# Rows loaded in one burst, x in four buffers, stores on a second queue: the end of a four-layer graph network on one core

## The chip, the cores and the metric

The kernel runs on one NeuronCore of one Trainium2 chip. The metric is the time of one execution on the device, in microseconds (us). Engines are named as the profile names them: PE is the matrix engine, DVE the vector engine, ACT the scalar engine, POOL is GpSimd, and SP is the sync engine, which here only issues transfers (DMAs).

## The reference

Eight graphs' node features `x` (8 batches of 2048 nodes with 64 features) pass through four layers that share one adjacency matrix. Each layer normalises x, applies ReLU, computes something of the graph, and adds it to x. The change lies in the last layer, which is graph attention, and above all in its last step:

```python
h = jnp.maximum(_layernorm(x, axis=-1), 0.0)
# _L3_gnn_ref(h, adj, weight, a, bias):
adj = adj.at[jnp.diag_indices(N)].set(1.0)
h = jnp.einsum('bni,io->bno', x, weight)
e_src = h @ a[:D, 0]
e_dst = h @ a[D:, 0]
e = jax.nn.leaky_relu(e_src[:, :, None] + e_dst[:, None, :], negative_slope=ALPHA)
e = adj[None, :, :] * e
attention = jax.nn.softmax(e, axis=-1)
h_prime = jnp.einsum('bij,bjd->bid', attention, h)
return h_prime + bias
# the last line of the whole network:
x = x + _L3_gnn_ref(...)
```

## The kernel before

**Layout.** x is held transposed: features of two batches on the 128 partitions, nodes along the free axis. So there are four pairs of batches (`NP = 4`), and the 2048 nodes are cut into four chunks (`NC = 4`) of 512 (`CW`), each of four tiles (`TC = 4`) of 128 nodes. One chunk of x is 128 x 4 x 512 floats, 1 MB. Between layers it lies in DRAM, in `xs[3][0..3]` for the last layer.

**The last layer.** For inputs such as these the kernel takes the branch `layer3_near`. In the last step of layer 2 the class `Scores` has already left, for every node, its projected features and two scores per batch in DRAM (`f_rows`, 2112 bytes a node; stored by SP at L1895 and L1896). The nodes are sorted by their number of neighbours, in an order read at the start of the layer (`order`, L1933). The class `Near` then goes over 15 tiles of 128 sorted nodes (`others`): POOL gathers the rows of each node and of its neighbours from `f_rows` into `ring` (L1959), DVE works out weights and multiplies, PE sums in PSUM, DVE divides. A sixteenth tile, that of the nodes with most neighbours, is done densely beside them (`first_tile`): its adjacency rows are gathered (L2060), ACT works out its exponentials, PE sums. What a tile gives is written by POOL to its nodes' places in DRAM, in `att_rows` (`put_back`, L1970).

**The end.** `result` (L2141) brings this back. Once all of `att_rows` is written, it loads 16 tiles of rows (`att(t)`, 128 x 512 floats, 256 KB each, L2150), transposes each by four PE instructions into PSUM (`pt`, two buffers, L2153), and adds it and the bias to x by one DVE instruction (L2155). When a chunk's four tiles are done, four stores of 256 KB take it to the output (L2159). x comes chunk by chunk into two halves of one buffer (L2145, L2146), so chunks 2 and 3 take the places of chunks 0 and 1. All these transfers are issued from SP, one after another.

**Memory.** `slots` hands out named stretches of SBUF, q0 to q5, of 16 KB a partition, that live through the whole kernel and are used again and again under new names: the end's x is in q2, its rows in q0 and q1. `w` is the last layer's own pool (`att`); its tiles lie one after another where layers 0 to 2 had theirs, and `ring` alone takes 76 KB a partition of it.

**Order of the work.** The tile framework sets the order of the instructions on each engine when it builds the program; it need not be that of the source. An engine then runs its own list strictly in order, and an instruction that waits holds up all behind it on that engine, transfers included. Semaphores between engines are placed by the framework from the tiles that instructions read and write.

Of the kernel before, what the change touches and what calls it, by code (L numbers as in the profile page):

```python
# [7 lines left out]
F = mybir.dt.float32  # L8
# [11 lines left out]
P = 128  # L20
# [3 lines left out]
NP = NB // 2  # L24
NT = N // P
R = P // NP
CW = 512
NC = N // CW
# [18 lines left out]
class Slots:  # L47
# [3 lines left out]
    def __init__(self, pool):  # L51
        self.flat = {f"q{i}": pool.tile([P, 2 * N], F, name=f"q{i}") for i in range(6)}
        self.pool = None
# [42 lines left out]
class Kernel:  # L96
# [1421 lines left out]
    def layer3_near(self, slots):  # L1518

        tc = self.tc
        with (
            tc.tile_pool(reuse_waits="tile", name="att", bufs=1) as w,
            tc.tile_pool(reuse_waits="tile", name="att_ps", bufs=1, space=PSUM) as ps,
        ):
            near = Near(self, slots, w, ps)
            first = near.first_tile()  # L1530
            others = near.others()
            next(first)
            next(others)
            for _ in range(12):
                next(first)
            for part in others:
                next(first, None)
            for part in first:
                pass
            near.put_back()  # L1540
            near.result()
# [369 lines left out]
class Near:  # L1911
# [5 lines left out]
    def __init__(self, kern, slots, w, ps):  # L1917
        self.kern, self.nc, self.w, self.ps = kern, kern.nc, w, ps
        nc = self.nc
        *_, self.y, self.total, self.rows = kern.last_slots(slots)  # L1920
        self.turn = 0
        self.x = slots.tile([P, 2, NP, CW], F, name="x_end", tag="q2")
        two = slots.tile([P, 2, N], F, name="first_row", tag="q0")
        self.row, self.whole = two[:, 0], two[:, 1].bitcast(I32)

        self.m = slots.tile([P, 4, NB, P], F, name="m", tag="q0")

        self.att = Halves(slots, "att", ("q0", "q1"), True)
        two = slots.tile([P, 2, N], F, name="first_at", tag="q1")
        self.first_at = two[:, 0].rearrange("p (t n) -> p t n", t=NT)  # L1930
        self.on_all = two[:, 1].rearrange("p (i b n) -> p i b n", i=2, b=NB)
        self.order = w.tile([P, 2, NT], I32, name="order")
        nc.sync.dma_start(self.order, kern.orders[1])  # L1933
        self.near = w.tile([P, FIRST[NT]], I32, name="near")
        nc.vector.tensor_scalar(self.near, kern.near, 1.0, -1.0, op0=OP.max, op1=OP.add)
        self.there = w.tile([P, FIRST[NT]], F, name="there")
        nc.vector.tensor_scalar(self.there, kern.near, 0.0, None, op0=OP.is_gt)
        self.ring = w.tile([P, self.RING, WIDE], F, name="ring")
        self.at, self.unread, self.back = 0, (), []
# [201 lines left out]
    def result(self):  # L2141

        nc, w, kern = self.nc, self.w, self.kern
        for ch in range(NC):
            x = self.x[:, ch % 2]  # L2145
            nc.sync.dma_start(x, kern.xs[3][ch])  # L2146
            for i in range(TC):
                t = ch * TC + i
                r = self.att(t)
                nc.sync.dma_start(r, kern.att_rows[t * P : (t + 1) * P])  # L2150
                pt = self.ps.tile([P, 4, P], F, name="pt", bufs=2)
                for q in range(NP):
                    nc.tensor.transpose(pt[:, q], r[:, q * P : (q + 1) * P], kern.ident)  # L2153
                here = x[:, :, i * P : (i + 1) * P]
                nc.vector.scalar_tensor_tensor(  # L2155
                    here, pt, kern.col("bias3"), here, op0=OP.add, op1=OP.add
                )
            for q in range(NP):
                nc.sync.dma_start(kern.a["out"][q, :, ch * CW : (ch + 1) * CW], x[:, q])  # L2159


def kernel(tc, a):
# [94 lines left out]
```

## Time and profile before

| What | us |
|---|---|
| median of 3 runs | 2223.89 (2223.14 to 2229.41) |
| the profiled execution | 2223.47 |
| its span in the profile | 2221.7 |
| PE busy | 1967.9 (89%) |
| DVE busy | 1115.2 (50%) |
| POOL busy | 727.9 (33%) |
| ACT busy | 708.9 (32%) |
| first gather of the last layer | 1929.7 |
| last write to `att_rows` issued | 2173.8 |
| first row load of `result` issued | 2176.65 |
| last output store issued | 2212.5 |

All times of instructions are counted from the start of the span. The span is what the profiler saw of the one execution; 1.8 us of the execution's own time lie around it. A line L135 in the profile is a helper through which nearly all matrix products go. Lines that begin with a time are the timeline: start, duration, engine, line, operation, and in brackets how long the engine was idle before it and what ended that. SPq is SP's list of transfers; a duration there is that of issuing them, and transfers next to one another are merged into one line with a count. A table by stages gives, for each stretch, every engine's busy time with its number of instructions, the clock that PE was granted, the mean busy share of the 16 DMA engines, and what they moved.

### The profile page before, as it was taken

The page shows a single profiled execution, that of the slowest core. Times are in us where ns is not written, and L with a number is a line of the kernel's source. Part 1 is how long each engine was busy: PE and PEld are TensorE (multiplying, and loading weights), DVE is VectorE, ACT ScalarE, POOL GpSimd, SP SyncE. Part 2 cuts the span into 40 slices and gives each one's busy share as a digit, 9 for nine tenths or more (in the row PEclk, how much of TensorE's full clock was granted, in tenths as well). Part 3 has the DMA queues.
Part 4 walks back from the last instruction along what each step waited for, and adds up shares of the span by engine and source line. Part 5 has one row for each costly group of instructions (what it writes and reads, how often), then busy time and mean ns, then how long its engine had stood idle before and what let it go on. Part 6 is the DMA issues. An engine that isn't in the chain of part 4 may idle for free.

```text
span 2221.7 us, 21410 instructions
## 1 busy us (share of the span) xinstructions
PE 1967.9 (89%) x7530; PEld 1187.1 (53%) x7530; DVE 1115.2 (50%) x1980; ACT 708.9 (32%) x1347; POOL 727.9 (33%) x609
## 2 busy tenths in 40 slices
PE   5877899987879989999999998998999999679873
PEld 1454766652226766353353532876777666345432
DVE  7846767744762032524425244988302222349762
ACT  6401455543444342020110200433434333258300
POOL 0012066755320002726537175011000000277760
PEclk8856899996777989999999998999999999789996
DMA  8231133451122453040130402456333443375655
GB/s 318 71 101 27 52 94 112 126 159 67 38 76 86 131 130 118 0 139 13 54 99 0 114 1 82 149 191 218 103 123 123 144 151 124 131 199 164 180 158 201
DMA packets 107742, 253.76 MB, mean 114 GB/s; under 512 B 19600, under 2 KB 19744, under 8 KB 100320
## 3 DMA queue, kind: packets, MB, share of 16 engines
q1 hardware_dynamic: 90000, 185.22, 26.1%
q0 software_dynamic: 17616, 67.00, 10.1%
q8 instruction: 63, 1.03, 0.2%
q14 instruction: 63, 0.52, 0.1%
HBM read 218.37 MB, written 33.81 MB: 114 GB/s over the span
## 4 chain that ended last, share of the span: by engine, by line
PE 57%; DVE 8%; POOL 7%; DMA 6%; issue 5%; ACT 3%; SPq 1%; POOLq 0%; DVEq 0%; ACTq 0%
PE pp L135 25%; PE pk L135 16%; PE bank L135 4%; POOL ring L1959 3%; PE acc L135 3%; PE pn L135 2%; PE p L135 2%; POOL q L1794 1%; DVE q L1809 1%; DMA q<-in_adj_dram,order 1%; POOL dt L632 1%; DMA adj_t<-in_adjT_dram 1%; PE pd L135 1%; PE po L135 1%; DMA ring<-f_rows,near 1%
## 5 line engine op out<-in xcount | busy, mean ns | idle before, releaser
L294 ACT CAST adj<-adj_t 128x512 fp32r<-128x512 f32 x384 | 236.7, 619 | 718.3 <-PE pp L135 625.2
L1353 POOL TENSOR_TENSOR acc<-acc,y 128x512 f32<-128x512 f32 x224 | 277.4, 1271 | 444.9 <-DVE y L1348 444.9
L135 PE MATMUL pk<-q,w 128*128 128x512 f32 (+1 forms) x1024 | 358.2, 612 | 9.9 <-DVE w L1270 8.9
L135 PEld LDWEIGHTS pk<-q,w 128*128 128x128 f32 (+1 forms) x1024 | 136.6, 188 | 228.0 <-issue 179.1
L135 PE MATMUL acc<-q,ident 128*128 128x512 f32 x416 | 205.1, 620 | 30.0 <-DVE q L2049 19.1
L1348 DVE SCALAR_TENSOR_TENSOR y<-pk,bias,q 128x512 f32<-128x512 f32 x224 | 157.7, 746 | 139.9 <-PE pk L135 130.3
L135 PE MATMUL pp<-adj,u_n_hi 128*128 128x512 f32 x768 | 217.2, 402 | 0.0
L135 PE MATMUL pp<-adj,u_n_lo 128*128 128x512 f32 x768 | 214.2, 398 | 0.0
L135 PEld LDWEIGHTS pp<-adj,u_n_hi 128*128 128x128 f32 x768 | 143.4, 188 | 39.0 <-issue 5.9
L1959 POOL DMA_INDIRECT ring<-f_rows,near x121 | 141.4, 1169 | 69.2 <-issue 57.4
L135 PEld LDWEIGHTS pp<-adj,u_n_lo 128*128 128x128 f32 x768 | 144.6, 188 | 34.5
L135 PEld LDWEIGHTS acc<-q,ident 128*128 128x128 f32 x416 | 77.1, 196 | 106.3 <-issue 48.8
L2063 POOL IOTA q<- 128x2048 int32 x1 | 1.8, 1835 | 355.3 <-PE p L135 355.3
L1794 POOL TENSOR_TENSOR q<-q,beta 128x512 f32<-128x512 f32 x57 | 67.6, 1188 | 104.8 <-DVE beta L1770 81.6
L135 PE MATMUL pp<-adj,x_ind_hi 128*128 128x512 f32 x256 | 95.5, 489 | 2.1 <-DVE q L700 1.9
L1348 DVE SCALAR_TENSOR_TENSOR acc<-pk,bias,q 128x512 f32<-128x512 f32 x32 | 22.6, 746 | 143.6 <-PE pk L135 143.6
L135 PE MATMUL bank<-std,from_rows 32*128 32x512 f32 x128 | 47.7, 938 | 41.8 <-DVE std L242 33.8
L135 PE MATMUL pp<-adj,h_n_hi 128*128 128x512 f32 x256 | 77.7, 416 | 0.0
L135 PE MATMUL pp<-adj,h_n_lo 128*128 128x512 f32 x256 | 75.3, 407 | 0.0
L2030 DVE TENSOR_TENSOR q<-ring,e 128x1024 f32<-128x1024 f32 x58 | 69.9, 1217 | 9.9 <-PE acc L135 9.7
L135 PE MATMUL pp<-adj,ah_n_hi 128*128 128x512 f32 x256 | 73.1, 405 | 0.0
L1416 DVE TENSOR_TENSOR q<-pn,later 128x512 f32<-128x512 f32 x32 | 21.5, 687 | 101.6 <-PE pn L135 101.4
(382 smaller groups left out, 3216.7 us busy)
## 6 DMA issues: line engine op xcount, KB each, us to landing
adj_t<-in_adjT_dram SPq DMA_DIRECT2D x160, 512.0 KB, 3.8
rows<-in_adj_dram SPq DMA_DIRECT2D x16, 1024.0 KB, 5.6
adj_t<-in_adjT_dram SPq DMA_DIRECT2D x64, 256.0 KB, 3.0
q<-x SPq DMA_DIRECT2D x12, 1024.0 KB, 5.0
q<-in_embT_dram SPq DMA_DIRECT2D x8, 1024.0 KB, 12.2
x<-q SPq DMA_DIRECT2D x8, 1024.0 KB, 3.9
x_ch<-in_xT_dram SPq DMA_DIRECT2D x4, 1024.0 KB, 6.2
h_rows<-q SPq DMA_DIRECT2D x16, 256.0 KB, 2.9
```

The costliest lines, as they stand in the source:

```text
L135: self.nc.tensor.matmul(out, lhsT, rhs, start=start, stop=stop)
L294: nc.scalar.copy(moving, at[:, i])
L632: nc.gpsimd.tensor_sub(dt, th[0], th[1])
L1348: nc.vector.scalar_tensor_tensor(y, pks[b, half], bias[:, b : b + 1], emb[:, b], op0=OP.add, op1=OP.mult,)
L1353: nc.gpsimd.tensor_add(acc, acc, y)
L1416: nc.vector.tensor_add(to, pn, later[:, 2].unsqueeze(1).to_broadcast(full))
L1794: self.nc.gpsimd.tensor_tensor(x, x, by.unsqueeze(2).to_broadcast([P, NB, D]), op=OP.mult)
L1809: nc.vector.tensor_add(d, d, self.pas.pop(i - 1))
L1959: self.nc.gpsimd.indirect_dma_start(to, None, self.kern.f_rows[:], bass.IndirectOffsetOnAxis(ap=index, axis=0))
L2030: nc.vector.tensor_tensor(y.rearrange("n i (b f) -> n i b f", b=NB), block[:, i : i + 2, : NB * D].rearrange("n i (b f) -> n i b f", b=NB) ...
L2063: nc.gpsimd.iota(whole, pattern=[[1, N]], base=0, channel_multiplier=0)
```

## The change

Four edits are made, all in the last layer. First, `result` issues the loads of all 16 tiles of rows ahead of its loop over chunks, not one by one inside. Second, x gets four buffers: the two halves in q2 as before, and a second tile of the same size, `x_more`, 16 KB a partition, which is allocated from `w` ahead of that pool's other tiles. Third, the four loads of x move from `result` to `layer3_near`, behind the first steps of the dense tile. They remain on SP. Fourth, the output is stored from ACT's queue and no longer from SP's.

```diff
@@ layer3_near
             next(others)
             for _ in range(12):
                 next(first)
+            for ch in range(NC):
+                tc.nc.sync.dma_start(near.x[ch], self.xs[3][ch])
             for part in others:
                 next(first, None)
             for part in first:
@@ Near.__init__
         *_, self.y, self.total, self.rows = kern.last_slots(slots)
         self.turn = 0
-        self.x = slots.tile([P, 2, NP, CW], F, name="x_end", tag="q2")
+        x = slots.tile([P, 2, NP, CW], F, name="x_end", tag="q2")
+        more = w.tile([P, 2, NP, CW], F, name="x_more")
+        self.x = [x[:, 0], x[:, 1], more[:, 0], more[:, 1]]
         two = slots.tile([P, 2, N], F, name="first_row", tag="q0")
@@ Near.result
         nc, w, kern = self.nc, self.w, self.kern
+        for t in range(NT):
+            nc.sync.dma_start(self.att(t), kern.att_rows[t * P : (t + 1) * P])
         for ch in range(NC):
-            x = self.x[:, ch % 2]
-            nc.sync.dma_start(x, kern.xs[3][ch])
+            x = self.x[ch]
             for i in range(TC):
                 t = ch * TC + i
                 r = self.att(t)
-                nc.sync.dma_start(r, kern.att_rows[t * P : (t + 1) * P])
                 pt = self.ps.tile([P, 4, P], F, name="pt", bufs=2)
@@
             for q in range(NP):
-                nc.sync.dma_start(kern.a["out"][q, :, ch * CW : (ch + 1) * CW], x[:, q])
+                nc.scalar.dma_start(kern.a["out"][q, :, ch * CW : (ch + 1) * CW], x[:, q])
```

## The prediction

> **What bounds the kernel now.** I read the page first, for the span and the chain of work that ended last.
>
> ```profile
> span 2221.7 us, 21410 instructions
> ...
> PE 57%; DVE 8%; POOL 7%; DMA 6%; issue 5%; ACT 3%; SPq 1%; POOLq 0%; DVEq 0%; ACTq 0%
> ```
>
> PE carries 57% of the chain, in layers 0 to 2, which the change does not touch. It can act at two places: at the end, where `result` runs, and at the start of the last layer, where the loads of x are to go. For the end I took SP's timeline from 2176 us on, then the table by stages.
>
> ```profile
> 2176.65 4.90 SPq L2150 DMA_DIRECT2D q<-att_rows  x9
> 2184.97 5.44 SPq L2159 DMA_DIRECT2D out_dram<-q  x8
> 2190.58 0.45 SPq L2146 DMA_DIRECT2D q<-x  x1
> 2191.07 1.92 SPq L2150 DMA_DIRECT2D q<-att_rows  x3
> 2193.83 0.32 SPq L2146 DMA_DIRECT2D q<-x  x1
> 2194.19 1.47 SPq L2150 DMA_DIRECT2D q<-att_rows  x2
> 2202.51 1.80 SPq L2159 DMA_DIRECT2D out_dram<-q  x4
> 2204.36 1.25 SPq L2150 DMA_DIRECT2D q<-att_rows  x2
> 2210.97 2.01 SPq L2159 DMA_DIRECT2D out_dram<-q  x4
> ```
>
> SP's list is strictly in order, and here it makes the steps of the end. The last scatter into `att_rows` lands at 2176.5 and row loads begin at once, nine of them. Then SP stands at the stores of chunk 0 until DVE has made them (2184.97), and goes on to the stores of chunk 1. Only behind these do x's chunk 2 (2190.58), three rows, chunk 3 (2193.83), two rows; the last two rows wait behind chunk 2's stores until 2204.36.
>
> ```profile
> 2180.00:2185.00 5.00, 4.32 (x18) 3.01 (x17) 3.00 (x4) 0.00 (x0) 0.00 (x0) 0.50 0.98 349
> 2185.00:2190.00 5.00, 3.38 (x17) 2.38 (x16) 2.91 (x4) 0.00 (x0) 0.00 (x0) 0.78 0.76 284
> 2190.00:2195.00 5.00, 0.00 (x0) 0.00 (x0) 0.00 (x0) 0.00 (x0) 0.00 (x0) 0.56 1.05 309
> 2195.00:2200.00 5.00, 1.35 (x7) 1.38 (x8) 0.97 (x2) 0.00 (x0) 0.00 (x0) 0.50 0.99 377
> 2200.00:2205.00 5.00, 3.58 (x15) 2.48 (x13) 2.78 (x4) 0.00 (x0) 0.00 (x0) 0.50 0.75 289
> 2205.00:2210.00 5.00, 1.84 (x9) 1.57 (x8) 1.41 (x2) 0.00 (x0) 0.00 (x0) 0.50 0.60 193
> 2210.00:2215.00 5.00, 0.16 (x1) 0.00 (x0) 0.84 (x2) 0.00 (x0) 0.00 (x0) 0.50 0.61 210
> ```
>
> PE and DVE do nothing from 2190 to 2195: rows are queued behind stores. The DMA engines are not idle then (share 1.05): they load the two chunks of x. Their share falls to 0.6 after 2205. The DMA view from 2176 to 2216 gives the rate:
>
> ```profile
> q1 hardware_dynamic: 4873, 10.45, 75.1%
> ```
>
> 10.45 MB in 75.1% of 40 us, so 30.0 us of all engines: **348 GB/s while busy**. In one-us slices the last busy one ends near 2215.2, where the last store lands. The remaining 6.5 us to 2221.7 are the program's end.
>
> For the other place, SP's timeline around 1906 and the one of all engines from 1925:
>
> ```profile
> 1906.10 12.35 SPq L2146 DMA_DIRECT2D q<-x  x2
> ...
> 1925.45 0.38 SPq L1896 DMA_DIRECT2D f_rows<-scores  x1
> 1925.89 0.93 SPq L1933 DMA_DIRECT2D order<-order  x1
> ```
>
> ```profile
> 1929.69 0.95 POOL L1959 DMA_INDIRECT ring<-f_rows,near  x1 [28.42 <-issue]
> ...
> 1937.03 2.35 DVE L2067 SCALAR_TENSOR_TENSOR q<-q,own 128x2048 f32<-128x2048 int32 x1 [8.35 <-DMA q<-in_adj_dram,order]
> 1937.21 2.99 POOL L1959 DMA_INDIRECT ring<-f_rows,near  x1 [0.30 <-issue]
> ```
>
> The two loads at 1906.10 (L2146; the second from 1918.0) are x's chunks 0 and 1. So these are early already; only chunks 2 and 3 can be gained by "early". SP waits there 11.6 us for DVE to finish with q2's second half, ahead of the last stores into `f_rows`. Tiles of `w` come later: `order` is the first of SP's, after the last `f_rows` store, and DVE's first work in `w` follows its last of layer 2 (1924.97 after 1924.90). POOL's first gather follows at 1929.69.
>
> **What the Trainium skill says.** (1) "DMA: Bandwidth & Descriptors", section "Issuing engines are not separate DMA queues": transfers from SP, ACT and POOL run on the same 16 engines, so another queue saves the sequencer's issue time only. Before has no transfer on ACT, so the sharing is unseen; SP's issue time is 446 ns at the median for a store and 464 for a row. What ACT's queue can also save here is the waiting ahead of the rows. (2) The same page, "Specifications", has about 358 GB/s as a core's share of memory bandwidth; the 348 above agree, so I take the end as bounded by bytes. (3) Its "Queues, rings and completion order": an engine takes turns between queues, packet by packet. So stores on ACT's queue slow the rows still loading on SP's, and loads of x on SP's slow POOL's gathers. No trace of before shows two such queues full together. (4) "SBUF — State Buffer", "SBUF: two separate sides": DVE and GpSimd share a port pair as a lock. The trace agrees: the gather at 1937.21 takes 2.99 us for a usual 0.95 while DVE's L2067 (2.35 us) runs. It is not a sign of full DMA queues, and moves with L2067.
>
> **The end, part by part.** Bytes left after 2176.5: rows 16 x 262,144 = 4.19 MB and stores as much, 8.39 MB. The two chunks of x, 2.10 MB, are gone from here. Four pace-setters:
> - DMA: 8.39 MB / 348 GB/s = 24.1 us. The first row reaches PE at 2179.3, and its own 0.75 us at that rate put the start of the flow near 2178. Without a break the last byte lands at 2202.1.
> - PE and DVE: the first eight rows start on DVE from 2180.44 to 2187.9, 1.07 us apart (PE at half clock 1.0, DVE 0.75 beside it). Sixteen: 2180.44 + 15 x 1.07 + 0.75 = 2197.2.
> - SP: 16 x 0.464 = 7.4 us, to 2184.1, ahead of the need.
> - ACT: idle at the end (0.00 in every stage); four stores behind the last DVE work, 4 x 0.446 = 1.8 us, and 2.7 us to land: 2201.7.
>
> Do the rows come in time under sharing? Until 2184.5 they have the engines alone: 2.26 MB, nearly nine rows. Then chunk 0's stores take half and a row lands every 1.5 us: row 15 near 2195, when PE wants it at 2195.3. No wait of size. DMA then sets the end with 2202.1; I add 1 us for gaps, as nothing starts a store before its DVE work. With 6.5 us behind it, 2209.6 in place of 2221.7: **12.1 us saved**. Half of it is x's 2.10 MB (6.0 us), the rest idle DMA time.
>
> The row loads wait for the last scatter as before, so "together" gains nothing at 2176.65. In the program as built, SP's transfers use eight completion semaphores in turn, and each waits for the one eight earlier. With stores from ACT in the same turn, a late row may wait for a store: from 0 to some 3 us more; I take 0, since PE and DVE pace those rows anyway.
>
> **The start of the last layer.** Chunks 0 and 1 keep their place, since q2's halves come free as before. `x_more` lies in `w`, so I expect its two loads on SP right behind `order`, at about 1926.9: 2 x 0.32 us of issue, with nothing queued behind them on SP until the rows at 2176. Their 2.10 MB run 6.0 us, until about 1934.5, beside POOL's first gathers. POOL issues one each 1.26 us and doesn't wait for landings of 3.9 us. Who waits is DVE: L2067 starts at 1937.03 when the dense tile's adjacency rows (1 MB, issued 1930.95) land. Of the 6.0 us, some 3.6 are over when these begin to flow; the rest shares by halves: about 2.4 us late. DVE is idle in 8.8 us of the 10 from 1970 to 1980, waiting for gathers, and the chain runs through POOL's issues there; that cover takes it up. Bounds: 0 and 6.0 us (all of it exposed); I take 0.6. `ring` and the rest of `w` move up by 16 KB; as they wait for the end of layer 2 already, I cost this at 0, between minus and plus 1.
>
> Sum: 12.1 - 0.6 = 11.5 us. From the profiled execution's 2223.47 that gives 2212.0; the median of the runs is 0.42 above it, so **2212.4 us**.
>
> **Rivals.**
> - *The early loads are exposed.* Should they stand ahead of `order` or of the last `f_rows` stores in SP's list, POOL's start is late by their 6.0 us and nothing takes that up: 2218.4. For it: SP already puts x ahead of `f_rows`. Against: `w` opened late in before.
> - *The end has holes.* Stores cut the rows to half their rate for longer and semaphores hold late rows; PE waits, and the last stores slip by 5 us: about 2217.4. For it: the rate under two queues is unseen.
> - *Slower: the last layer is laid out otherwise.* The interleaving of the dense tile with the 15 others is fixed at build, and new transfers and another memory layout may shift it. The stage lasts 247 us and holds single waits of 12.1 us (DVE's L2004, ending 1985.8) and 23.8 us (ACT's L2014). One more of these on the path decides from 12.1 us on; at 23.8 it gives about 2236. Against: only SP's list is edited.
> - *The change does less than it says.* Nine rows were together already, and x's first half was early. This is in the sum.
>
> **Chances.** Main case 0.62 (own range 2208 to 2216), exposed loads 0.13, holes 0.13, slower 0.07, better than the main case 0.05 (a faster DMA rate with reads and writes mixed: one-us slices of before reach 438 GB/s, 19 us in place of 24). A measurement can tell about 0.3%, here 6.7 us. The two middle rivals lie at that edge, half on each side: faster 0.80, same 0.13, slower 0.07. Range 2206 to 2219.
>
> **What the profile will show.** Right: SP issues 16 rows in one piece from about 2176.6, with no store among them; 16 stores stand on ACT; the last is issued near 2198; DMA share stays near 1 from 2180 to 2200; PE has no hole of 5 us. Two loads of x follow `order` near 1927; the first gather stays near 1929.7, L2067 starts by 2.4 us later, and the last scatter within 2 us of 2173.8. Wrong: a last scatter beyond 2178 (start or layout), or a last store beyond 2202 with DMA shares under 0.8 (holes).

## The result, and the profile after

| What | before | after |
|---|---|---|
| median of the runs, us | 2224.51 (2219.67 to 2229.41, 6 runs) | 2211.79 (2205.18 to 2215.03, 6 runs) |
| the profiled execution, us | 2223.47 | 2211.97 |
| its span, us | 2221.7 | 2210.2 |

The ratio is 0.9939, with a 95% interval of 0.992 to 0.9958: the kernel is faster by 0.6%. The forecast was 2212.4 us.

All comparisons below cut the span into three. **Start** runs to the first gather into `ring`, **middle** from there to the issue of the last scatter into `att_rows`, **tail** from that issue to the end of the span. Start and middle are long and differ by some us from one execution to the next. The tail varies less: in the six profiled executions below whose ends are built alike (after twice, the two edits, the small write, three and six loads) it was 35.07 to 37.18. It holds nearly all that the change does. Each figure for a part of the span comes from one execution.

| | start | middle | tail |
|---|---|---|---|
| before | 1929.69 | 244.09 | 47.92 |
| after | 1933.35 | 240.99 | 35.86 |

The tail is 12.06 us shorter. SP's timeline of the kernel after, from the start of the last layer on (start, duration, engine, line, operation):

```profile
1929.55 0.93 SPq L1937 DMA_DIRECT2D order<-order  x1
1930.53 0.90 SPq L1537 DMA_DIRECT2D x_more<-x  x2
2177.20 12.95 SPq L2149 DMA_DIRECT2D q<-att_rows  x16
```

and ACT's, for the same execution:

```profile
2185.68 8.14 ACTq L2163 DMA_DIRECT2D out_dram<-q  x8
2193.93 6.28 ACTq L2163 DMA_DIRECT2D out_dram<-x_more  x8
```

The two loads of `x_more` stand right behind `order`. At the end SP has one list of sixteen rows and nothing else. The steps that SP's stores made in before are gone. In the waits of before's end PE stood 21.8 us for rows, in five waits, the longest 10.0. In the waits of after's end (us in total, times, longest) there are two, the one for the first row and a short one:

```profile
PE pt L2157 <- DMA q<-att_rows: 7.5, 2, 6.8
```

The table by stages of after (engines' busy time, granted clock of PE, DMA share, GB/s):

```profile
2180.00:2185.00 5.00, 4.05 (x17) 3.29 (x18) 2.36 (x4) 0.00 (x0) 0.00 (x0) 0.50 1.00 349
2185.00:2190.00 5.00, 4.62 (x25) 3.14 (x25) 4.47 (x7) 0.00 (x0) 0.00 (x0) 0.79 0.90 328
2190.00:2195.00 5.00, 3.26 (x21) 2.15 (x22) 3.75 (x6) 0.00 (x0) 0.00 (x0) 1.00 1.04 390
2195.00:2200.00 5.00, 0.54 (x4) 0.30 (x4) 1.26 (x2) 0.00 (x0) 0.00 (x0) 0.74 0.97 357
```

The DMA share is near 1 from 2180 to 2200, while PE and DVE run out of work near 2196: the end is now bounded by bytes. (Shares a little above 1 stand in the view as they are; I read them as full.) The DMA view of after from 2170 to 2211 gives the rate (packets, MB, share of 16 engines):

```profile
q1 hardware_dynamic: 2304, 4.20, 29.1%
q10 hardware_dynamic: 2304, 4.20, 27.6%
```

q1 carries the rows, q10 the stores: 8.40 MB in 56.7% of 41 us, so 23.2 us of all engines, 361 GB/s. In that view's slices of about one us the last busy one ends near 2202.3.

At the start, the timeline of POOL and DVE of after:

```profile
1933.35 0.95 POOL L1963 DMA_INDIRECT ring<-f_rows,near  x1 [28.18 <-issue]
...
1942.04 2.41 DVE L2071 SCALAR_TENSOR_TENSOR q<-q,own 128x2048 f32<-128x2048 int32 x1 [9.71 <-DMA q<-in_adj_dram,order]
```

The dense tile's first DVE work starts 8.69 us behind the first gather; in before that distance was 7.34.

### The profile page after: what moved, and what is told of

The parts are those of the page before. It is cut to its first block, busy times and chain, and to the rows that moved or that the text cites. A ratio compares the mean times of both kernels' runs of the same rounds, so it can differ in the third digit from the quotient of the medians.

```text
span 2210.2 us, 21391 instructions
## 1 busy us (share of the span) xinstructions
PE 1962.3 (89%) x7530; PEld 1183.9 (54%) x7530; DVE 1115.4 (50%) x1980; ACT 709.2 (32%) x1347; POOL 724.2 (33%) x609
## 4 chain that ended last, share of the span: by engine, by line
PE 58%; DVE 9%; POOL 6%; DMA 5%; issue 5%; ACT 3%; SPq 0%; ACTq 0%; POOLq 0%; DVEq 0%
PE pp L135 26%; PE pk L135 16%; PE bank L135 4%; POOL ring L1963 3%; PE acc L135 3%; PE p L135 2%; PE pn L135 2%; POOL q L1796 1%; DVE q L1811 1%; DMA q<-in_adj_dram,order 1%; POOL dt L632 1%; PE pd L135 1%; DMA ring<-f_rows,near 1%; PE pt L1227 1%; PE po L135 1%
## 5 line engine op out<-in xcount | busy, mean ns | idle before, releaser
L2067 POOL IOTA q<- 128x2048 int32 x1 | 1.8, 1835 | 354.8 <-PE p L135 354.8
```

The lines of the kernel that those rows point to most:

```text
L2067: nc.gpsimd.iota(whole, pattern=[[1, N]], base=0, channel_multiplier=0)
```

## The experiments

The theory to be tested was the prediction's: the gain is x's bytes taken out of the tail and DMA idle time filled, one half each. The rivals: one of the two edits does it all; the second queue is what counts; the early loads cost something at the start. Each diff is against the kernel after. In the expectations, quoted as they were put on record, e2 is the run with the row and store edits alone, e3 the one with all but the second queue, e7 and e8 are those with the early loads three and six times, and e9 and e10 are the two repeats. What the runs left, with the medians of their own runs and the ratio to runs of before on the same chip:

| kernel | tail, us | median, us | ratio, 95% interval |
|---|---|---|---|
| x edits alone | 40.10 | 2216.61 | 0.9967, 0.9956 to 0.9979 |
| row and store edits alone | 47.68 | 2225.54 | 1.0006, 0.9992 to 1.002 |
| all but the second queue | 34.95 | 2210.43 | 0.9937, 0.9917 to 0.9958 |
| four buffers and ACT's stores alone | 35.90 | 2210.46 | 0.9945, 0.9932 to 0.9959 |
| `x_more` loaded behind the rows | 46.76 | 2223.26 | 0.9987, 0.9971 to 1.0003 |
| `x_more` loaded just ahead of the rows | 40.19 | 2222.12 | 0.998, 0.9959 to 1.0001 |
| early loads three times | 35.89 | 2216.18 | 0.997, 0.9955 to 0.9984 |
| early loads six times | 35.89 | 2230.44 | 0.9955, 0.9938 to 0.9972 |
| after, on that chip | 35.07 | 2228.36 | 0.9944, 0.9923 to 0.9965 |
| all but the second queue, on that chip | 34.09 | 2227.38 | 0.9936, 0.9921 to 0.9951 |

The last three rows are from one chip on which before's median was 2240.1 us; on the others it was 2223.7 to 2225.5.

### The edits of x alone

```diff
-        for t in range(NT):
-            nc.sync.dma_start(self.att(t), kern.att_rows[t * P : (t + 1) * P])
...
+                nc.sync.dma_start(r, kern.att_rows[t * P : (t + 1) * P])
...
-                nc.scalar.dma_start(kern.a["out"][q, :, ch * CW : (ch + 1) * CW], x[:, q])
+                nc.sync.dma_start(kern.a["out"][q, :, ch * CW : (ch + 1) * CW], x[:, q])
```

> Only the x edits: four buffers, early loads; row loads inside the loop and stores on SP as before. In the list of SP, nine rows, eight stores, seven rows, eight stores. Measured in the tail, from the issue of the last scatter into att_rows to the end of the span (before 47.9 us, changed 35.9). Theory Q (the end is paid in bytes of x and in rows that stand behind stores): 2.1 MB less, but seven rows still wait for two chunks' stores, so a tail of 38 (37 to 40), whole time near 2214. Rival B (only the bytes of x count): 36, near 2212. Rival S (the second queue brings the gain): 46 to 48, near 2223.

The tail is 40.10 us, just above the range of theory Q and 4 us from that of rival B. So 7.8 us are saved of 12.06. SP's timeline of this kernel shows what is left:

```profile
2181.07 5.08 SPq L2153 DMA_DIRECT2D q<-att_rows  x9
2189.22 4.90 SPq L2162 DMA_DIRECT2D out_dram<-q  x8
2194.16 3.70 SPq L2153 DMA_DIRECT2D q<-att_rows  x7
```

Seven rows still stand behind the first eight stores, to 2194.16. But with x gone they go out in one piece; in before the last two waited behind chunk 2's stores as well. So the removal of x's loads saves more than their bytes.

Before's own trace shows what else x cost. The ninth row, the first of chunk 2, was among the first nine loaded, and PE had transposed it by 2188.65 (36 transposes since 2179.29, four a row):

```profile
2187.99 0.66 PE L2153 MATMUL pt<-ident,q 128*128 128x128 f32 x4 [0.27 <-DVE q L2155]
...
2198.02 0.75 DVE L2155 SCALAR_TENSOR_TENSOR q<-pt,cols,q 128x512 f32<-128x512 f32 x1 [9.43 <-DMA q<-att_rows]
```

DVE added it at 2198.02 only. The view names a row's load as what ended that wait, but this row was there. The addition reads the row, the bias and x, so what it lacked was x's chunk 2, whose load SP had issued at 2190.58, behind eight stores. So DVE's long wait in before was one for x; PE's, up to 2198.65, was one for the next row, whose load stood behind those stores and that load of x.

### The edits of rows and stores alone

```diff
-            for ch in range(NC):
-                tc.nc.sync.dma_start(near.x[ch], self.xs[3][ch])
...
-        x = slots.tile([P, 2, NP, CW], F, name="x_end", tag="q2")
-        more = w.tile([P, 2, NP, CW], F, name="x_more")
-        self.x = [x[:, 0], x[:, 1], more[:, 0], more[:, 1]]
+        self.x = slots.tile([P, 2, NP, CW], F, name="x_end", tag="q2")
...
-            x = self.x[ch]
+            x = self.x[:, ch % 2]
+            nc.sync.dma_start(x, kern.xs[3][ch])
```

> The other two edits without x's: rows issued together, stores on ACT, x in two buffers and loaded in result, so that chunks 2 and 3 are loaded in the tail, behind all rows. Theory Q: 10.5 MB in the tail at 350 to 360 GB/s are 29 to 30 us from about 2178.5, and 7 us behind them: a tail of 42 (40 to 44), whole time near 2218. Rival B: 48, no gain. Rival S: 36, all of the gain.

The tail is 47.68 us: the other half of the change, by itself, saves 0.2 us. Theory Q's 40 to 44 was wrong. The number is rival B's, but B's 36 for x's edits alone did not come, so neither had the cause. SP's timeline of this kernel:

```profile
2183.39 13.75 SPq L2145 DMA_DIRECT2D q<-att_rows  x16
2200.53 7.77 SPq L2148 DMA_DIRECT2D q<-x  x2
```

and its waits at the end:

```profile
DVE q L2156 <- DMA out_dram<-q: 12.0, 1, 12.0
```

The rows are all there early, but x's chunk 2 is not. Its place is free only when chunk 0's stores have landed, and its load then goes out behind all that ACT and SP have queued. DVE stands 12.0 us. The view names the stores of chunk 0, which the load of x had to wait for; x itself was issued at 2200.53, its loads took up to 7.2 us to land, and DVE went on at 2208.04. The wait for rows has become a wait for x.

### x in its own buffers, but loaded behind the rows

Two things hold x in the run above: the buffer and the place in the queue. Here chunks 2 and 3 have buffers of their own; a one-column copy from the first row holds their loads until the tail, where they are issued behind the sixteen rows.

```diff
-            for ch in range(NC):
+            for ch in range(2):
...
+        for ch in range(2, NC):
+            nc.vector.tensor_copy(self.x[ch][:, 0, :1], self.att(0)[:, :1])
+            nc.sync.dma_start(self.x[ch], kern.xs[3][ch])
```

> The changed kernel with x's chunks 2 and 3 in their own buffer x_more, but loaded in the tail: a small DVE copy from the first row tile into x_more holds both loads until that tile has landed, and on SP they stand behind all 16 rows. So e2's bytes in the tail without e2's wait for the stores of chunks 0 and 1 to free q2. Theory R (e2 lost by the wait for its buffer; bytes alone cost their DMA time): the tail of the changed kernel, 35.9, plus 2.10 MB at 361 GB/s, 5.8 us: 41.7 (40 to 43), whole time near 2217. Rival (any load of x in the tail costs all, as bytes behind the rows): 47 to 48, near 2223.

The tail is 46.76 us: without the wait for the buffer, it is only 0.9 us below the run before this, less than like tails differ. Theory R (40 to 43) was wrong: the bytes alone don't explain the loss. SP's timeline:

```profile
2182.21 14.50 SPq L2149 DMA_DIRECT2D q<-att_rows  x16
2198.01 2.24 SPq L2152 DMA_DIRECT2D x_more<-x  x2
```

its waits,

```profile
DVE x_more L2162 <- DMA x_more<-x: 11.9, 1, 11.9
```

and its stages:

```profile
2200.00:2205.00 5.00, 0.00 (x0) 0.00 (x0) 0.00 (x0) 0.00 (x0) 0.00 (x0) 0.50 1.05 401
2205.00:2210.00 5.00, 3.17 (x14) 2.65 (x15) 2.97 (x5) 0.00 (x0) 0.00 (x0) 0.50 0.41 173
2210.00:2215.00 5.00, 2.48 (x12) 1.72 (x10) 2.85 (x4) 0.00 (x0) 0.00 (x0) 0.79 0.72 265
```

The DMA engines are full until x has landed; then comes a chain, transpose, addition, store, in which they are busy at 0.41 and 0.72. DVE begins chunk 2 at 2206.0, 23.8 us behind the first row's issue; in after this distance is 11.9 (2189.14 less 2177.20). Those 11.9 us, less 1.0 that the end makes up, are the 10.9 us between the tails.

### The same bytes, ahead of the rows

If the place is what costs, the same 2.10 MB should cost little more than their own time when they go first. Copies from the last tile's output hold the two loads until just before the rows.

```diff
-            for ch in range(NC):
+            for ch in range(2):
...
+            if place + 1 == len(self.TILES):
+                for ch in range(2, NC):
+                    nc.vector.tensor_copy(self.x[ch][:, 0, :1], o[:, :1])
+                    nc.sync.dma_start(self.x[ch], kern.xs[3][ch])
```

> The kernel after, but the last two chunks of x (2.10 MB) are loaded just ahead of the sixteen rows instead of beside the first gathers: a copy from the last tile's output into their buffers holds the loads until about 3 us before the rows. The same bytes are in the tail as in the run with x_more loaded behind the rows (tail from the last scatter's issue to the end 46.8 us, time 2223.3); only their place in the queue differs. Theory P (place): what those runs lost beyond x's bytes was lost because x stood at the end of a full queue and a serial chain of chunk, addition and stores followed it. Then here the tail is after's 35.9 us plus x's 5.8 us at the queue's rate, less up to about 3 us that x moves beside the last scatter: 38 to 40 us, and the time 2214 to 2216 us. Theory B (bytes): any x moved in the tail costs about 11 us wherever it stands: tail 46 to 48 us, time about 2223 us. A tail under 37 us would say that x's bytes cost next to nothing when they go first.

The tail is 40.19 us, just above what the place theory gave (38 to 40) and 6.6 below the run with the loads behind. SP's timeline of this kernel:

```profile
2178.84 0.80 SPq L2050 DMA_DIRECT2D x_more<-x  x2
2187.12 13.23 SPq L2153 DMA_DIRECT2D q<-att_rows  x16
```

The last scatter is issued at 2178.91. The rows follow 8.2 us later, where it was 2.9 in after: the scatter lands late among x's transfers. That puts the rows 5.3 us back; the end makes up 1.0 of it, and x costs 4.3 us (40.19 less 35.86). Part of x's 5.8 us of transfer (at 361 GB/s) lies beside the scatter's own landing, where the DMA engines had been idle, so 4.3 us is the price of this place and not of the bytes everywhere. The flow behind the scatter is unbroken: DMA shares of 1.05, 1.02 and 1.01 in the three stages from 2195 to 2210.

The median time, 2222.12 us, is 6 us above what the tail would give (2211.79 and 4.3), and doesn't tell the two theories apart. In the profiled execution 4.0 us of the difference to after lie in the middle (245.02), where the two kernels differ in nothing but the absent early loads and, at its very end, two one-column copies; the middles of the other kernels, on the chips where before took 2223.7 to 2225.5, range from 240.99 to 244.92. Why the time was high is open; the verdict here rests on the tail.

### All but the second queue

```diff
-                nc.scalar.dma_start(kern.a["out"][q, :, ch * CW : (ch + 1) * CW], x[:, q])
+                nc.sync.dma_start(kern.a["out"][q, :, ch * CW : (ch + 1) * CW], x[:, q])
```

> The whole change, but the stores stay on SP; its list is then 16 rows, 16 stores. Theory Q: no row stands behind a store and no x is loaded, so the tail is that of the changed kernel, 36 (35 to 38), near 2212: the queue of ACT isn't needed once the rows come first. Rival S: without the second queue 44 to 48, near 2222.

The tail is 34.95 us, as short as after's; rival S gave 44 to 48. SP's timeline:

```profile
2176.41 9.68 SPq L2149 DMA_DIRECT2D q<-att_rows  x16
2186.48 5.30 SPq L2163 DMA_DIRECT2D out_dram<-q  x8
2192.01 5.82 SPq L2163 DMA_DIRECT2D out_dram<-x_more  x8
```

and its stages:

```profile
2190.00:2195.00 5.00, 3.57 (x23) 2.15 (x21) 4.47 (x7) 0.00 (x0) 0.00 (x0) 1.00 1.05 404
2195.00:2200.00 5.00, 0.00 (x0) 0.00 (x0) 0.00 (x0) 0.00 (x0) 0.00 (x0) 0.72 1.07 403
```

Once all the rows are ahead of all the stores, stores from SP hold up nothing. ACT's queue isn't needed for the gain. This agrees with the Trainium skill's "DMA: Bandwidth & Descriptors", section "Issuing engines are not separate DMA queues": another issuing engine saves sequencer time alone, and here (34.95 against 35.86) no such saving shows. Where rows still stand behind stores it saves a wait as well, as the next run shows.

### Four buffers and ACT's stores alone

The loads of x and of the rows stand in the source where they stood in before.

```diff
-            for ch in range(NC):
-                tc.nc.sync.dma_start(near.x[ch], self.xs[3][ch])
...
-        for t in range(NT):
-            nc.sync.dma_start(self.att(t), kern.att_rows[t * P : (t + 1) * P])
...
+            nc.sync.dma_start(x, kern.xs[3][ch])
...
+                nc.sync.dma_start(r, kern.att_rows[t * P : (t + 1) * P])
```

> Only two of the four edits: four buffers and stores on ACT. The row loads stand in the loop and the loads of x in result, as before. Engine by engine the order as built is that of the changed kernel. Theory Q: tail 36 (35 to 37), loads of x_more still right behind order, whole time near 2212 within the spread of runs. If the place of the loads in the source counts in another way, a tail over 38 or loads of x in the tail.

The tail is 35.90 us, and the order of every engine's instructions in the last layer is that of after. The loads go where their buffers and their data allow, not where the source has them. So two of the four edits, the loop of row loads and the place of x's loads, do nothing by themselves once the stores are on ACT. The stores on ACT do matter with the row loads in the loop: as built, they alone set this run apart from that with x's edits alone (40.10), a difference of 4.2. And with the stores on SP the loop of row loads matters: it is all that sets the run before this one (tail 34.95) apart from that with x's edits alone (40.10).

### What the early loads cost

Two attempts were made to see the price of the early 2.10 MB: a load in the middle of the stage, and more loads at the start. The first writes one column of `x_more` on DVE in tile 7 and loads behind it:

```diff
+            if place == 7:
+                for ch in range(2, NC):
+                    nc.vector.memset(self.x[ch][:, :, :1], 0.0)
+                    nc.sync.dma_start(self.x[ch], kern.xs[3][ch])
```

> The changed kernel with the two loads of x_more held back to the middle of the last layer by a small DVE write into x_more after the eighth tile. If the early loads delay the start through shared DMA engines: the dense tile's DVE work starts 7.3 to 7.7 us after the first gather as in before, not 8.7 to 9.2; the stage from first gather to last scatter stays within 241 to 244 us, tail 36. If the early loads cost the whole stage something, the stage falls below 241.

This says nothing of a load in the middle. The small write waits for nothing, the build put it at 1927.4, and the loads followed at 1928.75, right behind `order` as in after. One execution took 2214.34 us, with a tail of 37.18.

The second loads chunks 2 and 3 again and again (range 2: three times in all; range 5: six times):

```diff
+            for _ in range(2):
+                for ch in range(2, NC):
+                    tc.nc.sync.dma_start(near.x[ch], self.xs[3][ch])
```

> The changed kernel with the two early loads of x_more issued three times, so 6.3 MB in place of 2.1 beside the first gathers, 17 to 18 us of all DMA engines in place of 6. Theory (the start's delay is taken up by DVE's idle time of 8.8 us near 1970 to 1980, as POOL's issues set the pace): the dense tile's DVE work starts some 11 to 13 us after the first gather, yet the stage from first gather to last scatter stays at 241 to 245; whole time within 3 us of the changed kernel. Rival (exposed): a stage of 250 to 256, whole time near 2222.

> The changed kernel with the two early loads of x_more issued six times: 12.6 MB beside the first gathers, some 35 us of all DMA engines. In e7 POOL already waited for landings at four gathers (2.6 us together) and reached its first scatter 54.6 us after the first gather, not 51; the stage still took 242.6. With twice the excess POOL and DVE must lose more than is idle: the dense tile's first DVE work as in e7, 11 us after the first gather, POOL's first scatter past 60 us, the stage at 246 to 255 if there is little slack behind, whole time 2217 to 2226. If the stage stays at 241 to 245 even so, the start of this layer is not on the path at all, and e7's higher time comes from elsewhere.

With 6.3 MB the dense tile's first DVE work starts 11.0 us behind the first gather (8.69 in after), and in POOL's waits up to 1990 five gathers now wait for the landing of an earlier one, 4.1 us in all. The profiled execution's middle is 242.62 us all the same, no longer than without these loads, and its tail 35.89. The median of the runs is 2216.18 us, 4.4 above after's, and the intervals of the two ratios barely touch (0.9955 and 0.9958). So a loss of some us is likely here, more than the 3 us that the expectation allowed. The profiled execution was the fastest of them, 2207.31 us, so where the others spent those us no trace shows.

With 12.6 MB POOL's first scatter comes 60.3 us behind the first gather. That distance is 51.4 us in before, 51.0 in after, and 56.5 and 57.5 in the two other kernels of that chip (next section). The middle is 252.81, inside what was expected for little slack. But those two kernels, with 2.10 MB alone, have 265.15 and 259.42, so this middle can't be set down to the loads. The median time is 0.9955 of before's, and the interval overlaps that of after on the same chip, which is 2.1 us faster at the median. If the 4.4 us for 4.2 MB more were a price in proportion to the bytes, the 2.10 MB would cost some 2 us (an estimate), and five times 2.10 MB more would have cost 11 us on that chip, where 2.1 were seen. The two runs don't fit one price. Whether the 2.10 MB cost anything stays open; a price of that size is below what these runs can see.

### The two fastest again

After and the version with all stores on SP ran once more beside the run with six loads.

> The changed kernel once more, for a comparison on the same chip with e8 and e10: 2208 to 2214, tail 36, stage 241 to 244.

> The variant of e3 once more: rows first, stores behind them on SP. Its tail was 34.95 against 35.86 and 35.90 with the stores on ACT, since the rows then have the DMA engines for themselves until the last is issued. If that holds, 0.5 to 1.5 us below e9, a tail of 35; if not, the same as e9.

Both ratios repeat (0.9944 and 0.9936). The tail with the stores on SP is again about 1 us shorter, 34.09 against 35.07, after 34.95 against 35.86. In the times that is no difference that can be told: the intervals overlap for the most part. That the rows gain from having the DMA engines to themselves is not shown. On this chip the middle was 265.15 and 259.42 us; PE's longest wait there was 12.3 us in after's execution and 13.8 in the other's, each for nothing that the profile shows.

## Why the prediction was right, and the step that was not

**The sum at the end: right.** 12.1 us were forecast and 12.06 came. The end is bounded by bytes over rate, as reckoned; that the number fits so closely is luck. Its terms: the rate was 361 GB/s and not 348 (23.2 us of transfers, not 24.1); the first row was issued at 2177.20, 0.55 later, since the last scatter was (2174.34); the last store landed near 2202.3, where 2202.1 was said. Counted from the last scatter's issue, that is 28.0 us, where 29.3 were forecast with the 1.0 for gaps. Behind it came 7.9 us, where 6.5 were said. Two misses of about 1.4 us cancel.

**The split of it: wrong.** "Half of it is x's 2.10 MB (6.0 us), the rest idle DMA time" has two terms that can be had one by one. The runs show that they can't: x's edits alone save 7.8, the others alone 0.2, both together 12.06. The step that failed is the reading of the hole from 2190 to 2195, "rows are queued behind stores". DVE's row was there, and DVE waited for x's chunk 2 until 2198.02. In before, rows and x both stood behind stores in SP's list, and each holds the last chunks in part. With x early and the rows still behind stores, 4.2 us of the gain are lost (40.10 less 35.86). With the rows free and x late, x stands behind sixteen rows and holds DVE for 12.0 us, and 11.8 of the 12.06 are lost. x's price is not its bytes' 6.0 us either. Ahead of the rows x costs 4.3, partly hidden beside the last scatter, behind them 10.9, because a chain of addition, transposes and stores then starts only when the queue has emptied. I had costed them as bytes, without asking when the work that needs them could start.

**The second queue: right on the price, silent on the need.** I wrote that it saves issue time and the waiting ahead of the rows. It is one of two ways to get the rows past the stores; issuing them first is the other, and with that ACT's queue gained nothing (34.95 against 35.86). With the rows in the loop it is worth 4.2 (40.10 against 35.90).

**SP's issue: 7.4 us were said, 12.95 measured.** In SP's own waits 4.6 us of it are six waits of a row's load for an earlier row's landing, the completion semaphores used in turn that I had bounded at some 3 us and taken at 0: more than the bound. No wait for a store, the one that I had feared, shows. It did little harm, as argued: past the first row PE waited 0.7 us for rows. In all, DVE ended at 2196.3, where 2197.2 was said, with PE's clock at 1.00 from 2190 to 2195. ACT was slower than said: it had issued its last store by 2200.2, 3.9 us behind DVE's last work and not 1.8. The bytes ended at 2202.3 anyway.

**The start: right, with a smaller delay.** The two loads came right behind `order`, as expected. The chip with the longer times apart, five kernels load `x_more` early and once (after, x alone, stores on SP, two edits, the small write). In these the dense tile's DVE work starts 8.07 to 9.18 us behind the first gather, 8.81 at the mean. In before and the three that load x's last chunks at the end (behind the rows, ahead of them, in two buffers) it starts after 7.34 to 7.66, 7.52 at the mean. It is late by 1.3 us, where 2.4 was said. The middle is 241.0 to 243.8 us in the one group and 241.1 to 245.0 in the other. So no loss from the delay shows, though one of its size, and the 0.6 us that I charged, would not be seen in this spread. The slow gather moved with DVE's work, as said: in after it is the one at 1943.39, 1.89 us, and it ends 0.83 us behind L2071, as it ended 0.82 behind L2067 in before. But the gather at 1942.13 took the usual 0.95 us although L2071 had begun at 1942.04, so the trace bears out the lock only in part.

**The total: right partly by chance.** Two terms of the profiled execution that the change doesn't explain came out opposite: the first gather at 1933.35, 3.66 later than in before and not "near 1929.7", and a middle 3.10 shorter. Their sum, 0.56, happens to be the 0.6 that I had charged to the start. That the span met the forecast to 0.1 us owes something to that. That the medians agree, over six runs each, owes less to it.

**The rivals.** Early loads exposed: no, they stand behind `order`. Holes at the end: none, the DMA share is 0.90 or more in every stage from 2180 to 2200. The slower one, a last layer laid out otherwise: the order of PE, DVE, ACT and POOL there is the same in before and after, SP's and ACT's transfers apart. "The change does less than it says": true of two edits of the four, as the run with the other two shows, whose tail and time are after's.

## What to carry to other kernels

At the end of a kernel, count the bytes that can't move before the last producer is done, divide by the rate that the trace shows, and make everything else early; then look in each issuing engine's list for a load that stands behind a store that waits. Edits that free different waits in one list in order need not add up (here 7.8 and 0.2 us alone, 12.06 together), so price them together and test them apart. When an engine waits for several things, ask of each whether it was there: the view names only one. A transfer behind a full queue costs its bytes and the chain that starts when it lands: here 10.9 us for 2.10 MB, in place of 4.3 where they went first.

## What the runs showed that was not expected

- With all transfers from SP, the DMA engines moved 403 and 404 GB/s in two stages of 5 us, the second of which is stores alone (the last row is issued by 2186.1, and a row takes at most 5.8 us to land). The Trainium skill's "DMA: Bandwidth & Descriptors", section "Specifications", which the prediction leaned on, has about 358 for a core, a stack's bandwidth halved between two cores. Here one core runs, and the measurement goes beyond it. So before's 348, close to that figure, was no sign that stores can't go faster. Over the whole end the same kernel comes to after's 361.
- A load that is free to go was put early by the build wherever the source had it, and so was a small write meant to hold it back. Only data that it must wait for held it.
- The same kernels took some 16 us longer on one of the chips, before and after alike, and in two of the three executions profiled there PE stood 12.3 and 13.8 us in the last layer for a reason that the profile doesn't show. The cause is open. The ratios were unmoved.
